# An adaLN block on one core: leads that change over time in the planner that orders all engines

## The chip, the core and the metric

The kernel runs on one core of a Trainium2 chip. The metric is the time of one execution on the device in microseconds (us); lower is better. Before the change three runs took 1426.54, 1429.36 and 1430.04 us, median 1429.36.

The core has five engines that take their own instructions, each in its written order, and wait for one another by semaphores: TensorE (PE; matmuls, with the weight loads shown apart as PEld), VectorE (DVE), ScalarE (ACT), GpSimd (POOL) and SyncE (SP, which issues the DMAs). TensorE writes its results to PSUM, which has eight banks here of 512 fp32 values in each of 128 partitions.

## The reference

For a batch of 8 sequences of 1024 tokens with 128 features, a modulated block: six linear-attention transformer layers between two residual sums, then a feed-forward part with values rounded to fp4.

```python
mod = (_silu(L0_c) @ L0_wmod).reshape(L0_c.shape[0], 6, 1, -1)
sa, ca, ga, sb, cb, gb = (mod[:, 0], ..., mod[:, 5])
ga = (2 * (ga >= 0) - 1) * jnp.maximum(jnp.abs(ga), 0.25)   # gb the same
h = _layernorm(x, axis=-1) * (1 + ca) + sa
x = x + ga * _L0_attn_ref(h, ...)      # six layers
h = _layernorm(x, axis=-1) * (1 + cb) + sb
x = x + gb * _L0_ffn_ref(h, ...)
```

One of the six layers:

```python
xn = _layernorm(x, ln1_w[i], ln1_b[i])
q, k, v = xn @ wq[i], xn @ wk[i], xn @ wv[i]          # 8 heads of 16
q = softmax(q, axis=-1); k = softmax(k, axis=-2)      # k: over the tokens
context = einsum('bhnd,bhne->bhde', k, v)
x = einsum('bhnd,bhde->bhne', q, context) @ wo[i] + bo[i] + x
xn = _layernorm(x, ln2_w[i], ln2_b[i])
hdn = leaky_relu(xn @ w1[i], 0.01)                    # 512 wide
x = hdn @ w2[i] + x
```

The feed-forward part takes its input, its weights and the gated product through a rounding to fp4 in blocks of 16 values with a scale of their own (largest absolute value / 6), then computes `silu(x @ gate.T) * (x @ up.T)`, 352 wide, and the projection back to 128. All matmuls are fp32.

## The kernel before

**Tiles.** One sequence of the batch is a tile of 128 partitions by 8 chunks of 128 features; most steps work on a half of it (4 chunks, 512 columns, one bank of PSUM). Four sequences are in flight at once, each in one of four sets of buffers ("lanes"; sequence b has lane b modulo 4), so sequences 4 to 7 start when 0 to 3 have left their buffers.

**Stages.** For a sequence there are eight stages: 0 is the first normalisation and modulation; 1 to 6 are the layers; 7 is the feed-forward part. A layer (`layer`) does, for each half: statistics of the norm (DVE L559, L561), its reciprocal root by logarithm and exponential on ACT and four small DVE steps (`layernorm`, L575 to L601), the normalised values (DVE L607, ACT L614), transposes on PE (`transposed`, L633), keys and queries (PE L867 and L914), their softmaxes (DVE L874, L923, L930, L943, L950; ACT L890, L937; POOL L955), keys times normalised input (PE L977), two small products (PE L986, L1011), the attention output (PE L1044, added by DVE L1029), and the two matmuls of the layer's own MLP (PE L1063, 512 columns; L1080, 128 columns, accumulated over four).

Stage 7 (`ffn`) normalises, rounds to fp4 (`fp4`: DVE L658 to L701, ACT L690, POOL L708), forms gate and up (PE L1120, ACT L1128 with the silu table, DVE L1136) in four quarters of two chunks, rounds each quarter to fp4, transposes it (PE L1151, ACT L1166), projects it down (PE L1177) and adds it to x (DVE L1186). "Quarter 4.3" below is quarter 3 of sequence 4. Each two quarters end in a store on SP's queue.

**The silu table.** ACT holds the tables of one set of functions. Gates need another set than the exponentials and logarithms of the layers, so each change between the two kinds costs a table load, shown as ACT_TABLE_LOAD at L1128 (to silu) or L1261 (back).

**The order.** The code does not run its steps as it writes them: it records each as a `Step` in a `Plan` (`add`), with its engine, an estimate of its duration and what it reads and writes. `order` then plays the whole program once while it is built. Of all steps whose inputs are there it takes the one that can start first; between steps that can start at the same time it takes the one with the largest sum of its `tail` (the longest chain of work behind it) and its `lead`. The steps are written to the engines in the order so found, and that order is fixed in the program. A step's lead is a number of its stage and sequence, from the table `LEAD` (8 sequences by 8 stages), so `LEAD` decides how the sequences in flight are interleaved. Set-up work that belongs to no stage (weights' preparation, loads, the modulations) has a lead of its own, set by `aside` and `load`.

**The fillers.** Where TensorE would stand idle for over 0.6 us in the played schedule, `order` puts matmuls of the identity by itself there (`warm`, L1250), as many as fit, if a bank of PSUM is free for them. Their result is never read.

```python
pick = (t + cost, -s.tail - s.lead, n, t, cost)
...
gap = e == "PE" and t - free[e] > self.GAP
while gap and min(bank_free) <= free[e]:
```

Of the kernel before, what the change touches and what calls it, by code (L numbers as in the profile page):

```python
# [37 lines left out]
class Buf:  # L38
# [4 lines left out]
    def __init__(self, pool, shape, tag, name, parts=1, dtype=F32):  # L43
        self.tag, self.make, self.tile = tag, (pool, shape, dtype, tag, name), None
        self.parts, self.after = [Part(self, i) for i in range(parts)], None
# [16 lines left out]
class Ps:  # L62


    n = 0
# [17 lines left out]
class Plan:  # L83
# [6 lines left out]

    def __init__(self):
        self.steps, self.wrote, self.read, self.on = [], {}, {}, {}
        self.lead, self.batch = 0.0, -1

    def add(self, eng, occ, fn, r=(), w=(), func=None, port=False):

        s = Step()
        s.eng, s.occ, s.fn, s.func, s.lead = eng, occ, fn, func, self.lead  # L100
        s.batch, s.port = self.batch, port or eng == "POOL"
        s.lat, s.n, s.deps, s.outs = self.LAT[eng], len(self.steps), set(), []
        s.ps = list(dict.fromkeys(x for x in (*r, *w) if isinstance(x, Ps)))
        for x in s.ps:
            x.users += 1

        def keys(things):
            for x in things:
                if isinstance(x, Buf):
                    yield from x.parts  # L110
                else:
                    yield x

        r, w = list(keys(r)), list(keys(w))
        for x in (*r, *w):
            if isinstance(x, Part):
                tag = x.buf.tag
                if x.buf.after is None:
                    x.buf.after = self.on.get(tag, set())
                    self.on[tag] = set()  # L120
                s.deps |= x.buf.after
                self.on[tag].add(s.n)
        for x in (*r, *w):
            if x in self.wrote:
                s.deps.add(self.wrote[x])
        for x in w:
            s.deps.update(self.read.get(x, ()))
        for x in r:
            self.read.setdefault(x, []).append(s.n)
        for x in w:  # L130
            self.wrote[x], self.read[x] = s.n, []
        s.deps.discard(s.n)
        for x in s.ps:


            if x.first is None:
                x.first = s
            else:
                x.first.deps.update(d for d in s.deps if d < x.first.n)
        self.steps.append(s)  # L140

    def order(self, warm):


        steps = self.steps
        for s in steps:
            for d in s.deps:
                steps[d].outs.append(s.n)
        for s in reversed(steps):
            s.tail = s.occ + s.lat + max((steps[o].tail for o in s.outs), default=0.0)  # L150
        free = dict.fromkeys(self.LAT, 0.0)
        free["PE"] = 1.8
        bank_free = [0.0] * BANKS
        left = [len(s.deps) for s in steps]
        ready = [0.0] * len(steps)
        cand = {e: {s.n for s in steps if s.eng == e and not s.deps} for e in free}
        table, port_free = None, 0.0
        out, todo = [], len(steps)
        while todo:
            banks = sorted(bank_free)  # L160
            best = None
            for e, c in cand.items():
                for n in c:
                    s = steps[n]
                    t = max(free[e], ready[n], port_free if s.port else 0.0)
                    need = sum(x.bank is None for x in s.ps)
                    if need:
                        t = max(t, banks[need - 1])
                    if t < INF:
                        cost = SWITCH if s.func and table and s.func != table else 0.0  # L170


                        pick = (t + cost, -s.tail - s.lead, n, t, cost)
                        if best is None or pick < best[1]:
                            best = (e, pick)
            assert best is not None
            e, (_, _, n, t, cost) = best
            gap = e == "PE" and t - free[e] > self.GAP
            while gap and min(bank_free) <= free[e]:
                to = free[e] + (2 if free[e] < self.COLD else 1) * mm(P)  # L180
                if to > t - self.BRINK:
                    break
                w, bank = Step(), bank_free.index(min(bank_free))
                w.fn, w.func = lambda bank=bank: warm(bank), None
                free[e] = bank_free[bank] = to
                out.append(w)
            s, todo = steps[n], todo - 1
            cand[e].discard(n)
            end = t + cost + s.occ
            table = s.func or table  # L190
            port_free = end if s.port else port_free
            for x in s.ps:
                if x.bank is None:
                    x.bank = min(range(BANKS), key=lambda i: bank_free[i])
                    bank_free[x.bank] = INF
                x.users -= 1
                if x.users == 0:
                    bank_free[x.bank] = end + s.lat
            free[e] = end
            for o in s.outs:  # L200
                ready[o] = max(ready[o], end + s.lat + self.SEE[steps[o].eng])
                left[o] -= 1
                if left[o] == 0:
                    cand[steps[o].eng].add(o)
            out.append(s)
        return out
# [21 lines left out]
def mm(n):  # L228

    return 0.01 + n * 1.66e-3  # L230


def move(kb):

    return max(0.45, kb * 4.0e-3)
# [6 lines left out]
def kernel(  # L242
# [38 lines left out]


    LEAD = [
        [1790.16, 1590.63, -133.39, -357.74, -170.79, -746.20, -949.01, -1084.50],
        [-328.73, -887.78, 125.60, 74.06, -1565.69, -372.37, -623.33, -863.15],
        [207.64, -149.66, -1586.32, -941.39, -1592.66, 94.98, -1452.11, -1239.07],
        [-746.08, 404.44, -824.95, -647.90, -118.96, -127.38, -1745.97, -425.45],
        [542.33, -1490.70, -1058.13, -1440.16, -391.61, -339.71, -149.19, -1160.38],
        [-1848.97, 2004.30, 268.43, 1104.45, -662.40, -326.99, -708.65, -1359.47],
        [573.17, -93.03, 284.47, -756.78, -278.27, -748.61, 318.91, -1786.29],  # L290
        [968.46, -558.77, 587.25, -611.65, -410.32, -941.76, -1400.05, -882.04],
    ]
    NQ = 4
    FCOLS = C // NQ * I

# [7 lines left out]
    plan = Plan()  # L303
    add = plan.add

    def stage(b, i):
        plan.lead, plan.batch = LEAD[b][i], b * len(LEAD[b]) + i

    @contextmanager
    def aside(late=40.0):  # L310

        kept = plan.lead, plan.batch
        plan.lead, plan.batch = -late, -2
        yield
        plan.lead, plan.batch = kept

    def chunks(t):
        return t.rearrange("p (c d) -> p c d", d=D)
# [1 line left out]
    def big(ln, which, name):  # L320

        return Buf(lanes_p, [P, W], f"{which}{ln}", name, 2 * H)
# [14 lines left out]

    def load(dst, src, key, kb=64):

        if plan.batch == -1:  # L340
            plan.lead -= 1e4
        add("SP", move(kb), lambda: nc.sync.dma_start(dst(), src), w=key)

# [20 lines left out]
    def load_x(b, h):  # L364
        if h == 0:
            x0s[b] = big(b % LANES, "x0", f"x0_{b}")
        src = x_d[b].rearrange("(p c) d -> p c d", c=C)[:, h * HC : (h + 1) * HC, :]
        load(lambda: chunks(half(x0s[b], h)), src, at(x0s[b], h), 256)
# [10 lines left out]
    for l in range(L):  # L379
# [13 lines left out]
        if l == 0:  # L393
            load_x(3, 0)
            load_x(3, 1)
    plan.lead = 0.0

    ident = const.tile([P, P], F32, name="ident")
    make_identity(nc, ident)
# [689 lines left out]
    def ffn(x, mod, b, ln):  # L1089
# [18 lines left out]
        )  # L1108
        G = C // NQ
        gs = []  # L1110
        for i in range(NQ):
            g = Buf(lanes_p, [P, W], f"{'CDEA'[i]}{ln}", f"g_{b}_{i}", G)
# [88 lines left out]
    for b in range(B):  # L1201
        ln = b % LANES
        stage(b, 0)
        mod = mod_buf(b, ln)
        if b < LANES:
# [5 lines left out]
        with aside():  # L1211
            modulation(mod, b, b < LANES)
        x = big(ln, "X", f"x_{b}")
# [39 lines left out]
    last, table = {}, None  # L1253
# [2 lines left out]
    behind = mybir.DependencyInfo(  # L1256
        mybir.DependencyClass.NoSync, mybir.DependencyReason.DATA
    )
    for step in plan.order(warm):
        if step.func == "exp" and table != "exp":  # L1260
            nc.scalar.preload_act_table_set("natural_log_exp_and_others")  # L1261
        table = step.func or table
        step.fn()
        new = block.instructions[done:]
        done += len(new)
        for i in new:
            if i.engine in last:
                tc.add_manual_dep(i, last[i.engine], behind, reason="order")
            last[i.engine] = i.name
# [40 lines left out]
```

## Time and profile before

| what | value |
|---|---|
| median of three runs | 1429.36 us |
| the profiled execution | 1430.2 us, its span 1428.5 us |
| TensorE busy | 1415.8 us, 9395 passes |
| VectorE / ScalarE / GpSimd busy | 1146.0 / 995.9 / 241.8 us |
| TensorE's clock, mean of what was granted | 0.999 |
| DMA | 18.81 MB, 13 GB/s over the span |

The span runs from the first to the last instruction of the profile, and the execution's own time is 1.7 us longer. An fp32 matmul takes two passes through TensorE, and the trace shows both, so most counts of its rows are twice the number of instructions; a transpose takes one pass. A matmul's own duration in a row runs from its start until its result is written; the next pass starts before that. Line numbers are those of the kernel before; in the changed kernel lines after the new table stand 37 further down.

### The profile page before, as it was taken

What the parts mean: (1) busy time and instruction counts of PE and PEld (TensorE: products, weight loads), DVE (VectorE), ACT (ScalarE), POOL (GpSimd) and SP (SyncE); (2) the same over time, 40 slices, a digit from 0 to 9 for tenths busy, and PEclk for the clock granted to TensorE, in tenths of its full rate; (3) what the DMA queues carried; (4) which work ended last, traced back from release to release, by engine and by line L of the source; (5) the groups of instructions that cost most, each with busy time, mean ns of one, the idle gap of its engine ahead of it and who ended that gap; (6) DMA issues with size and microseconds to landing.
All of it is one profiled execution on the core that took longest, in us unless ns stands there. A gap on an engine that the chain in (4) does not pass through costs nothing.

```text
span 1428.5 us, 26720 instructions
## 1 busy us (share of the span) xinstructions
PE 1415.8 (99%) x9395; PEld 1140.9 (80%) x9395; DVE 1146.0 (80%) x4560; ACT 995.9 (70%) x2280; POOL 241.8 (17%) x207
## 2 busy tenths in 40 slices
PE   9999999999999999999999999999999999999998
PEld 7787877878787887877787788878887877886887
DVE  7896776667787985798978978987796775989986
ACT  5776777566677777676776867785677677777763
POOL 2020101001121220112112212111221001222232
PEclk9999999999999999999999999999999999999999
DMA  7100000000000000000000000100000000000000
GB/s 214 47 1 1 1 1 1 1 1 1 1 22 6 16 1 1 1 27 16 1 1 28 8 1 8 27 1 8 9 1 1 1 1 1 1 16 1 16 16 15
DMA packets 16006, 18.81 MB, mean 13 GB/s; under 512 B 1552, under 2 KB 9848, under 8 KB 15872
## 3 DMA queue, kind: packets, MB, share of 16 engines
q1 hardware_dynamic: 15872, 17.10, 3.8%
q8 instruction: 74, 1.21, 0.3%
q14 instruction: 60, 0.49, 0.1%
HBM read 12.88 MB, written 4.22 MB: 12 GB/s over the span
## 4 chain that ended last, share of the span: by engine, by line
PE 82%; DVE 14%; ACT 2%; issue 1%; POOL 0%; DMA 0%; SPq 0%; DVEq 0%; POOLq 0%
PE ps L1080 23%; PE ps L1063 22%; PE ps L633 10%; PE ps L1044 5%; PE ps L977 5%; PE ps L914 5%; PE ps L867 5%; PE ps L1120 3%; PE ps L1177 2%; PE ps L1151 1%; PE warm L1250 1%; DVE x L1029 1%; DVE stats_m L559 1%; DVE nmax L874 1%; DVE qmax L923 1%; DVE stats_a L559 1%
## 5 line engine op out<-in xcount | busy, mean ns | idle before, releaser
L1063 PE MATMUL ps<-xT_m,w_sb 128*128 128x512 f32 x768 | 350.4, 595 | 1.5 <-ACT xT_m L847 1.4
L1063 PEld LDWEIGHTS ps<-xT_m,w_sb 128*128 128x128 f32 x768 | 137.5, 191 | 133.2 <-issue 91.9
L1029 DVE TENSOR_TENSOR x<-ps,x 128x512 f32<-128x512 f32 x192 | 129.5, 681 | 119.1 <-PE ps L1080 107.6
L955 POOL TENSOR_TENSOR q<-q,qsum 128x512 f32<-128x512 f32 x96 | 102.9, 1079 | 674.8 <-DVE qsum L950 374.6
L1080 PEld LDWEIGHTS ps<-w_sb,hT_D 128*128 128x128 f32 x768 | 103.9, 192 | 17.2 <-issue 13.6
L914 PEld LDWEIGHTS ps<-wq_sb,xT_a 128*128 128x128 f32 x768 | 96.6, 192 | 26.1 <-issue 16.8
L1080 PE MATMUL ps<-w_sb,hT_E 128*128 128x128 f32 x768 | 117.1, 275 | 0.0
L1080 PE MATMUL ps<-w_sb,hT_C 128*128 128x128 f32 x768 | 117.1, 275 | 0.0
L1080 PE MATMUL ps<-w_sb,hT_B 128*128 128x128 f32 x768 | 117.1, 275 | 0.0
L1080 PE MATMUL ps<-w_sb,hT_D 128*128 128x128 f32 x768 | 117.0, 275 | 0.0
L1080 PEld LDWEIGHTS ps<-w_sb,hT_B 128*128 128x128 f32 x768 | 101.4, 192 | 1.2 <-issue 0.7
L614 ACT ACTIVATE xh_a<-x,shift_a,rstd_a 128x128 f32<-128x128 f32 x192 | 83.8, 488 | 25.9 <-DVE shift_a L601 25.4
L1080 PEld LDWEIGHTS ps<-w_sb,hT_E 128*128 128x128 f32 x768 | 101.2, 192 | 0.0
L1080 PEld LDWEIGHTS ps<-w_sb,hT_C 128*128 128x128 f32 x768 | 101.2, 192 | 0.0
L914 PE MATMUL ps<-wq_sb,xT_a 128*128 128x128 f32 x768 | 99.0, 275 | 0.0
L1044 PEld LDWEIGHTS ps<-m,qT 128*128 128x128 f32 x768 | 91.1, 192 | 7.5 <-DVE m L1018 3.1
L867 PE MATMUL ps<-xT_a,wk_sb 128*128 128x512 f32 x192 | 96.7, 599 | 0.4 <-DMA wk_sb<-in_L_attn_wk_dram 0.2
L977 PEld LDWEIGHTS ps<-k,xh_a 128*128 128x128 f32 x768 | 90.7, 192 | 6.1 <-issue 4.5
L1044 PE MATMUL ps<-m,qT 128*128 128x128 f32 x768 | 95.1, 275 | 0.1
L575 ACT ACTIVATE rstd_a<-mv_a,eps 128x4 f32<-128x4 f32 x96 | 28.4, 297 | 93.9 <-DVE mv_a L561 80.4
L977 PE MATMUL ps<-k,xh_a 128*128 128x128 f32 x768 | 93.5, 275 | 0.0
L614 ACT ACTIVATE xh_m<-x,shift_m,rstd_m 128x128 f32<-128x128 f32 x192 | 81.8, 487 | 13.9 <-DVE shift_m L601 13.6
(176 smaller groups left out, 3132.5 us busy)
## 6 DMA issues: line engine op xcount, KB each, us to landing
x<-in_L_attn_x_dram SPq DMA_DIRECT2D x16, 256.0 KB, 3.2
out_dram<-x SPq DMA_DIRECT2D x16, 256.0 KB, 2.0
w_sb<-in_L_attn_w_dram SPq DMA_DIRECT2D x12, 256.0 KB, 3.9
mod<-mod_d SPq DMA_DIRECT2D x8, 256.0 KB, 4.3
mod<-mod_d SPq DMA_DIRECT2D x4, 128.0 KB, 3.3
wmod_b<-in_L_wmod_dram SPq DMA_DIRECT2D x1, 384.0 KB, 4.1
wk_sb<-in_L_attn_wk_dram SPq DMA_DIRECT2D x6, 64.0 KB, 3.0
wq_sb<-in_L_attn_wq_dram SPq DMA_DIRECT2D x6, 64.0 KB, 2.8
```

The costliest lines, as they stand in the source:

```text
L559: nc.vector.bn_stats(stats.ap()[:, c, :], s(c))
L614: nc.scalar.activation(d(c), s(c), AF.Identity, bias=shift.ap()[:, c : c + 1], scale=rstd.ap()[:, c : c + 1],)
L633: nc.tensor.transpose(t.ap()[:, c * P : (c + 1) * P], chunks(half(src, h))[:, c, :], ident)
L867: lambda tk=tk, h=h: nc.tensor.matmul(tk.ap(), wk_sb[:, l, :], half(xT, h), start=True, stop=True),
L914: nc.tensor.matmul(tq.ap()[:, c * D : (c + 1) * D], half(xT, h)[:, c * P : (c + 1) * P], wq_sb[:, l, :], start=True, stop=True,)
L955: lambda h=h, hs=hs: nc.gpsimd.tensor_tensor(heads(half(q, h)), heads(half(q, h)), each(qsum.ap()[:, hs]), ALU.mult),
L977: nc.tensor.matmul(tc_.ap()[:, :D], chunks(xh.ap())[:, c, :], chunks(k.ap())[:, c, :], start=(c == 0), stop=(c == C - 1),)
L1029: lambda: nc.vector.tensor_tensor(half(x, h), t.ap(), half(x, h), ALU.add),
L1044: nc.tensor.matmul(to.ap()[:, c * D : (c + 1) * D], half(qT, h)[:, c * P : (c + 1) * P], m.ap(), start=True, stop=True,)
L1063: lambda th=th, h=h, j=j: nc.tensor.matmul(th.ap(), w1_sb[:, l, j * P : (j + 1) * P], half(xmT, h), start=True, stop=True,),
L1080: nc.tensor.matmul(ty.ap()[:, c * D : (c + 1) * D], hidden(j)[:, c * P : (c + 1) * P], w2_sb[:, l, j, :], start=(j == 0), stop=(j == NJ - 1),)
L1120: lambda t=t, cc=cc, n=n: nc.tensor.matmul(t.ap()[:, :I], hT.ap()[:, cc * P : (cc + 1) * P], wguT[:, n, :], start=True, stop=True,),
```

## The change

The rank of a step no longer takes its lead from when it was recorded. A step keeps its stage, `(b, i)`, and `order` looks up the lead of that stage while it plays. It has a copy of the table, and a second table `TURNS` says at which times of the played schedule which entries take another value: at 15 us, sequence 2's stage 0 drops to -419, and so on in 27 entries up to 1365 us. `LEAD` itself is rounded to whole numbers; besides, sequence 3's stages 0 and 3 rise by 223 and 156, and sequence 4's row drops by 3 to 4. Set-up work without a stage ranks 70 us later than it did (`LATE`), apart from the loads at the start.

Nothing of what is computed changes, and no instruction of the chip is written differently: steps, tiles, buffers and durations in the planner are the same. What changes is the order in which they stand on each engine, the bank of PSUM that each gets, and with them how many fillers and table loads there are.

```diff
-        self.lead, self.batch = 0.0, -1
+        self.lead, self.stage = 0.0, None
...
-    def order(self, warm):
+    def order(self, leads, turns, warm):
...
-        table, port_free = None, 0.0
+        table, port_free, now = None, 0.0, 0.0
+        leads, turns = [list(x) for x in leads], list(turns)
         out, todo = [], len(steps)
         while todo:
+            while turns and turns[0][0] <= now:
+                for b, i, lead in turns.pop(0)[1]:
+                    leads[b][i] = lead
...
-                        pick = (t + cost, -s.tail - s.lead, n, t, cost)
+                        lead = leads[s.stage[0]][s.stage[1]] if s.stage else s.lead
+                        pick = (t + cost, -s.tail - lead, n, t, cost)
...
-            end = t + cost + s.occ
+            now = t + cost
+            end = now + s.occ
...
     LEAD = [
-        [-746.08, 404.44, -824.95, -647.90, -118.96, -127.38, -1745.97, -425.45],
-        [542.33, -1490.70, -1058.13, -1440.16, -391.61, -339.71, -149.19, -1160.38],
+        [-523, 404, -825, -492, -119, -127, -1746, -425],
+        [539, -1494, -1061, -1443, -395, -343, -152, -1163],
...
+    TURNS = [
+        (15, [(2, 0, -419)]),
+        (30, [(1, 0, -1058)]),
...
+        (1215, [(5, 7, -1015), (7, 5, -1033)]),
+        (1260, [(4, 7, -889), (5, 7, -174)]),
+        (1275, [(4, 7, -2229), (5, 7, -1786)]),
+        (1320, [(5, 7, -1788), (6, 7, -1804)]),
+        (1335, [(5, 7, -1863)]),
+        (1350, [(5, 7, -1786), (7, 7, -2743)]),
+        (1365, [(7, 7, -1661)]),
+    ]
+    LATE = 70.0
...
     def aside(late=40.0):
...
-        plan.lead, plan.batch = -late, -2
+        plan.lead, plan.stage = -LATE - late, None
...
-    for step in plan.order(warm):
+    for step in plan.order(LEAD, TURNS, warm):
```

## The prediction

> **What bounds the kernel now.** I read the page's busy shares first, then the chain of waits, then the matmuls grouped by line and shape, and last the windows that say where idle time lies.
>
> ```profile
> span 1428.5 us, 26720 instructions
> PE 1415.8 (99%) x9395; PEld 1140.9 (80%) x9395; DVE 1146.0 (80%) x4560; ACT 995.9 (70%) x2280; POOL 241.8 (17%) x207
> PE 82%; DVE 14%; ACT 2%; issue 1%; POOL 0%; DMA 0%; SPq 0%; DVEq 0%; POOLq 0%
> ```
>
> TensorE is idle for 1428.5 - 1415.8 = 12.7 us. It sets the end, so only two things can shorten the run: fewer passes on TensorE, or less time lost between them. An order changes no useful pass. But not all passes are useful: L1250 multiplies the identity by itself to fill a gap and its result is never read.
>
> ```profile
> L1250 PE MATMUL warm<-ident 128*128 128x128 f32 x388 | 49.8, 282 | 1.6 <-POOL ident masks.py:199 1.6
> ```
>
> The 282 ns is one pass from end to end; passes overlap, so the price is the pitch. The chain of waits in order of time gives it for each shape (start, duration, what):
>
> ```profile
> 1183.20 6.87 PE ps L1063 x16
> 1190.07 7.14 PE ps L1080 x64
> ...
> 1387.84 6.03 PE warm L1250 x54
> ...
> 1415.02 5.14 PE warm L1250 x46
> ```
>
> 6.03 / 54 = 0.1117 us a pass, and two passes a filler (388 records for 194 instructions): 0.2233 us a filler, 388 x 0.1117 = 43.3 us in all. In the same way the chain's rows give 0.1116 us for a useful 128-wide pass (7.14 us for 64 of L1080), 0.4294 for a 512-wide one (6.87 for 16 of L1063), 0.296 for L1120 (2.96 for 10), 0.109 for a transpose (2.18 for 20 of L633). Times the counts by line: 960 x 0.4294 + 5952 x 0.1116 + 256 x 0.296 + 1792 x 0.109 and about 6 of set-up = 1353 us of useful passes. So the span is 1353 useful + 43 filler + 32 of everything else (start, end, stalls). These 75 us are all that an order can touch.
>
> Where they lie, by windows of 50 us, fillers alone (length, PE busy and count, PEld busy and count, clock, DMA, GB/s):
>
> ```profile
> 0.00:50.00 50.00, 21.51 (x162) 20.07 (x162) 1.00 0.61 186
> 550.00:600.00 50.00, 2.86 (x20) 2.67 (x20) 1.00 0.00 1
> 1200.00:1250.00 50.00, 0.61 (x4) 0.53 (x4) 1.00 0.01 1
> 1300.00:1350.00 50.00, 1.28 (x10) 1.20 (x10) 1.00 0.03 11
> 1350.00:1400.00 50.00, 12.41 (x100) 11.93 (x100) 1.00 0.03 12
> 1400.00:1450.00 50.00, 11.09 (x92) 10.75 (x92) 0.99 0.03 11
> ```
>
> Start and tail, then; the middle has ten fillers. One stall of the middle has no filler: around 645 us TensorE waits 2.3 us behind a table load and three gates on ScalarE (L1128), and then runs at half clock:
>
> ```profile
> PE ps L633 <- ACT g L1128: 2.5, 2, 2.3
> ...
> 648.30:651.60 3.30, 3.30 (x6) 1.24 (x5) 2.46 (x4) 1.60 (x3) 2.47 (x3) 0.50 0.02 5
> ```
>
> The 3.3 us at clock 0.50 do 1.7 us of work less, so this stall costs 2.3 + 1.7 = 4.0 us.
>
> **What the Trainium skill says.** "TensorE: Matmul & The Clock Gate", Part 1: the clock halves after an idle window of about 3.4 us, and the windows run free. The trace shows the halving after only 2.3 us of full idleness, so shorter stalls can cost too. "Perfetto Trace Analysis", on the most-contended engine: matmul busy is a poor measure since matmuls are pipelined. The trace agrees: 99% busy hides 75 us, which is why I count passes by pitch. "ScalarE: Activation LUTs", on what a table load costs: about 1.28 us for the load and as much again for a drain; the trace shows 1.283 us for the load in each of its 37.
>
> **The change part by part.** The leads decide ties of the planner, which runs while the program is built; nothing of it runs on the chip. What can be read without a clock is the order of instructions that comes out.
>
> Useful work: the same 5,405 matmul instructions, the same DVE, POOL and SP operations; cost 0. ScalarE has two table loads less (35 for 37): 2.6 us on an engine with 30% idle, counted at nothing since TensorE sets the end; the cover is ScalarE's idle time, and if it is gone at such a place it costs what the stall at 645 us did.
>
> Fillers: 141 instead of 194, by place. Start, up to the 74th useful matmul: 75 for 81, -6. Middle: the ten after matmuls 2266 and 2282, and two after 4743, are gone, -12. Before batch 7's last feed-forward: 20 between matmuls 5125 and 5251 are gone; those after 5321 and 5333 are 14 for 32, together -38. In batch 7's own serial feed-forward: 52 for 49, +3. Sum -6 -12 -38 +3 = -53, and 53 x 0.2233 = 11.8 us less on TensorE.
>
> What takes their place is useful work moved, not created. Before, batches 4 and 5 finish their down projections at matmuls 4954 and 5171. After, quarters 4.1 and 4.2 come 104 and 76 matmuls later, 4.3 comes 259 later, 5.1, 5.2 and 5.3 come 90, 42 and 104 later, between the last layers of batch 7. What is late next at the end is batch 7's own chain of normalise, quantise, gate, quantise, project: 23 fillers in one gap there both before and after. That stays.
>
> Each moved quarter also moves its DVE chain: reduce 0.88, two small scalings 0.18 + 0.19, reciprocal 0.42, three sweeps of 0.88, add 0.42 = 4.7 us, plus 0.8 + 0.6 + 0.4 on ScalarE and 1.4 on POOL. Nothing is added in sum; it stands in windows where DVE is busy 42 to 46 of 50 us. I cost it at nothing, with DVE's idle share there as cover.
>
> DMA: the write of the small first modulation goes out four places earlier on SP's queue, ahead of feed-forward weights needed much later; DMA is idle (0.00 to 0.09 of a window past 50 us), cost 0. The result stores of batches 4 and 5 alternate. Behind a store that waits for 4.3 stands only 5's second one, then 6 and 7; these come later anyway. Cost 0. The 70 us by which set-up work ranks later show as another order of its matmuls (L505, L517) among batch 0's first layer; that is inside the -6.
>
> The unknown is the other 32 us: waits that the planner doesn't fill, because no bank of PSUM was free (645 us) or because they are short. The order doesn't show them. Bounds: -4 if the stall at 645 us isn't met again and no new one arises; +4 if there is another like it (17 of the 18 table loads for gates had none of over 1 us). I take -2, half of the stall.
>
> Sum: -11.8 - 2 = -13.8. The profiled execution took 1430.2 (span 1428.5 and 1.7 around it), which gives 1416.4; the three runs have a median 0.8 lower, 1429.4, so 1415.6. I say 1416.
>
> **The rivals.**
> A, the forecast: fillers leave, useful work closes up. For: TensorE is the bound and pitch is constant. 1416, between 1411 and 1421.
>
> B, the unfilled waits shrink as well. A tighter order lowers both kinds. TensorE's idle time between 50 and 1350 us is 4.3 us by the windows (2.4 of it at 645), the half clock 1.7; with all of it gone, 11.8 + 6 = 17.8 and about one more at the start: 1410. Against: some waits below a microsecond seem to be in any order.
>
> C, waits take the fillers' place. Every engine takes its instructions in the written order, so where data come later than planned, TensorE stands idle instead. For: behind some fillers TensorE idled on, 0.82 us for DVE's L1136 at 1361 us and 0.62 us for ScalarE's L847 at 1365. Seven places lose fillers; 0.6 to 1 us at each gives back 4 to 7: 1422. Against: long stretches of the middle have 50.00 of 50 busy without any filler.
>
> D, slower: DVE becomes the bound of the tail. The four quarters that move furthest (4.1, 4.3, 5.1, 5.3) carry 4 x 4.7 = 18.8 us of DVE. Between 1250 and 1400 us DVE is busy 42.75 + 46.27 + 42.55 = 131.6 of 150, which leaves 18.4. If the moved work came wholly from before 1250 it would fill this, and each further microsecond would delay batch 7's normalisation; if all 18.8 landed on its chain: 1429.4 - 11.8 + 18.8 = 1436. It decides once more than 11.8 us land there. Against: before, these quarters already ran at 1262 to 1338 us, inside the same window, so its sum hardly changes.
>
> **How the numbers follow.** A 0.69, B 0.13, C 0.12, D 0.06. Predicted is A, 1416. Its bounds give 1411 to 1421; B's low side and C's centre are taken in: 1409 to 1423. A measurement here can tell 0.3% (4.3 us) from no change. A and B are faster by more; of C a quarter falls within 0.3%, of D a third. Faster 0.69 + 0.13 + 0.09 = 0.91, same 0.05, slower 0.04.
>
> **What would show it.** The profile of the changed kernel should have 282 filler passes (388 before), PE still at 99%, useful passes at the same pitch, about 8 us less filler time past 1300 us and none in the middle. Each step is wrong if: idle time on TensorE rises by over 4 us (C), DVE between 1250 and 1400 shows no idle and L633 or L1063 wait for it (D), or a gate's table load again leaves TensorE idle with half clock after it (no -2). Useful passes at another pitch would break the whole sum.

## The result, and the profile after

The changed kernel takes 1419.13 us (median of 4 runs, 1418.68 to 1420.5), the kernel before 1429.66 us beside it (4 runs, 1426.54 to 1430.04). The ratio is 0.9933 with a 95% interval of 0.9915 to 0.995: 10.5 us less, where 13.8 were forecast. The profiled span goes from 1428.5 to 1417.8 us.

The page of the changed kernel, its span, busy shares and the chain of waits by engine:

```profile
span 1417.8 us, 26520 instructions
PE 1404.3 (99%) x9289; PEld 1127.9 (80%) x9289; DVE 1151.5 (81%) x4560; ACT 992.6 (70%) x2278; POOL 241.5 (17%) x207
PE 81%; DVE 12%; ACT 3%; DMA 2%; SPq 1%; issue 1%; POOL 1%; POOLq 0%
```

TensorE is still the bound. It is idle for 1417.8 - 1404.3 = 13.5 us (12.7 before), so no idle time was won; all of the gain is in what fills the busy time. Its passes are 106 fewer, and the groups by line show which:

```profile
L1287 PE MATMUL warm<-ident 128*128 128x128 f32 x282 | 36.8, 284 | 1.6 <-POOL ident masks.py:199 1.6
```

They are the fillers: 282 passes where there were 388. By windows of 50 us, fillers alone (length, PE busy and count, PEld busy and count, clock, DMA, GB/s), in the same windows as shown for the kernel before:

```profile
0.00:50.00 50.00, 20.58 (x150) 18.89 (x150) 1.00 0.62 186
550.00:600.00 50.00, 0.00 (x0) 0.00 (x0) 1.00 0.00 1
1200.00:1250.00 50.00, 0.00 (x0) 0.00 (x0) 1.00 0.00 1
...
1350.00:1400.00 50.00, 9.69 (x78) 9.35 (x79) 1.00 0.07 27
1400.00:1450.00 50.00, 6.52 (x54) 6.26 (x54) 0.98 0.03 11
```

Between 1300 and 1350 us there are none now, where there were 10. In sum 12 passes less at the start, 24 in the middle, 70 past 1300 us: with two passes a filler these are the 6, 12 and 35 instructions that the order had shown.

The waits of TensorE by who released them (us in total, times, longest):

```profile
PE ps L670 <- ACT g L1165: 2.3, 1, 2.3
PE warm L1287 <- POOL ident masks.py:199: 1.6, 1, 1.6
PE ps L670 <- DVE xh_a L644: 0.7, 3, 0.3
PE ps L951 <- ACT g L1165: 0.7, 1, 0.7
PE ps L1157 <- ACT g L1165: 0.7, 1, 0.7
```

The first row is the stall that I had half counted out: a transpose behind a table load and three gates, 2.3 us as before, at 640 instead of 645 us. The timeline of the changed kernel at that place (start, duration, engine, what, idle time before it):

```profile
636.51 4.31 PE L1157 MATMUL ps<-wguT,hTf 128*128 128x352 f32 x14
...
641.28 1.28 ACT L1165 ACT_TABLE_LOAD   x1
...
642.58 1.18 ACT L1165 ACTIVATE g<-ps 128x352 f32<-128x352 f32 x3
...
643.10 0.65 PE L670 MATMUL ps<-ident,xh_a 128*128 128x128 f32 x4 [2.28 <-ACT g L1165]
```

The trace of before has the same rows at this place with the same durations, 4.1 us later; the fillers that left ahead of it (6 at the start and 10 below 600 us, 16 x 0.2233) make up 3.6 of these. The input of the transposes is complete when ScalarE begins the table load (its L651 ends just ahead of it), and the row names a gate as releaser: what TensorE waits for is the bank of PSUM that the first gate empties, and the table load stands ahead of that gate. That holds for the last 1.8 of the 2.3 us at least; in the first 0.4 us ScalarE is still writing the input. What is different is the clock after the stall. The window of 3.4 us that follows the stall in the changed kernel (PE, PEld, DVE, ACT, POOL busy, then the clock):

```profile
643.10:646.50 3.40, 3.40 (x14) 1.97 (x14) 3.40 (x6) 2.63 (x5) 2.77 (x2) 1.00 0.00 0
```

1.00, where it was 0.50 before. Whether the change did that is asked by the experiments.

Two readings are left. DVE between 1250 and 1400 us, where the moved quarters land:

```profile
1250.00:1300.00 50.00, 49.69 (x328) 39.95 (x328) 48.62 (x172) 41.88 (x89) 8.03 (x7) 1.00 0.02 7
1300.00:1350.00 50.00, 49.35 (x321) 39.30 (x320) 46.74 (x144) 36.25 (x75) 15.72 (x12) 1.00 0.00 1
1350.00:1400.00 50.00, 48.43 (x322) 39.45 (x321) 42.20 (x107) 26.69 (x57) 15.21 (x11) 1.00 0.07 27
```

137.6 of 150 us, 6.0 more than before and 12.4 short of full. And the end of the chain of waits (start, duration, what): the program still closes with the serial feed-forward of batch 7 and its fillers.

```profile
1390.61 5.00 PE ps L1157 x16
1395.61 3.79 PE warm L1287 x34
...
1401.61 2.68 PE ps L1214 x24
1404.29 5.14 PE warm L1287 x46
...
1411.52 2.69 PE ps L1214 x24
```

### The profile page after: what moved, and what is told of

The parts are those of the page before. It is cut to its first block, busy times and chain, and to the rows that moved or that the text cites. A ratio compares the mean times of both kernels' runs of the same rounds, so it can differ in the third digit from the quotient of the medians.

```text
span 1417.8 us, 26520 instructions
## 1 busy us (share of the span) xinstructions
PE 1404.3 (99%) x9289; PEld 1127.9 (80%) x9289; DVE 1151.5 (81%) x4560; ACT 992.6 (70%) x2278; POOL 241.5 (17%) x207
## 4 chain that ended last, share of the span: by engine, by line
PE 81%; DVE 12%; ACT 3%; DMA 2%; SPq 1%; issue 1%; POOL 1%; POOLq 0%
PE ps L1100 20%; PE ps L1117 19%; PE ps L670 11%; PE ps L1014 6%; PE ps L951 6%; PE ps L904 5%; PE ps L1081 5%; PE ps L1157 4%; PE ps L1214 2%; DVE x L1066 1%; PE ps L1188 1%; DVE stats_a L596 1%; PE warm L1287 1%; DMA w_sb<-in_L_attn_w_dram 1%; DVE stats_m L596 1%
## 5 line engine op out<-in xcount | busy, mean ns | idle before, releaser
L1117 PEld LDWEIGHTS ps<-w_sb,hT_D 128*128 128x128 f32 x768 | 103.9, 192 | 17.2 <-issue 13.2
L1117 PE MATMUL ps<-w_sb,hT_E 128*128 128x128 f32 x768 | 117.1, 275 | 0.0
L1117 PE MATMUL ps<-w_sb,hT_C 128*128 128x128 f32 x768 | 117.1, 275 | 0.0
L1117 PE MATMUL ps<-w_sb,hT_B 128*128 128x128 f32 x768 | 117.1, 275 | 0.0
L1117 PE MATMUL ps<-w_sb,hT_D 128*128 128x128 f32 x768 | 117.0, 275 | 0.0
L651 ACT ACTIVATE xh_a<-x,shift_a,rstd_a 128x128 f32<-128x128 f32 x192 | 83.9, 489 | 29.2 <-DVE shift_a L638 28.5
L1117 PEld LDWEIGHTS ps<-w_sb,hT_B 128*128 128x128 f32 x768 | 101.3, 192 | 1.0 <-issue 0.5
L1117 PEld LDWEIGHTS ps<-w_sb,hT_C 128*128 128x128 f32 x768 | 101.2, 192 | 0.0
L1117 PEld LDWEIGHTS ps<-w_sb,hT_E 128*128 128x128 f32 x768 | 101.2, 192 | 0.0
L651 ACT ACTIVATE xh_m<-x,shift_m,rstd_m 128x128 f32<-128x128 f32 x192 | 82.3, 488 | 16.3 <-DVE shift_m L638 15.8
```

What stands on the lines that cost most here:

```text
L651: nc.scalar.activation(d(c), s(c), AF.Identity, bias=shift.ap()[:, c : c + 1], scale=rstd.ap()[:, c : c + 1],)
L1117: nc.tensor.matmul(ty.ap()[:, c * D : (c + 1) * D], hidden(j)[:, c * P : (c + 1) * P], w2_sb[:, l, j, :], start=(j == 0), stop=(j == NJ - 1),)
```

## The experiments

The question was threefold: is a filler worth its pitch, was the stall at 640 us (and the half clock) in the hands of the change, and does the gain come from the turns or from the other edits. In the table, "rest" is the span of the profiled run less 1353 us of useful passes (11.6 more in `extra_passes`), less filler passes x 0.1117 us.

| kernel | median us (runs) | span | filler passes | rest |
|---|---|---|---|---|
| before | 1429.66 (4) | 1428.5 | 388 | 32.2 |
| before_again | 1429.0 (1) | 1427.3 | 388 | 31.0 |
| changed | 1419.13 (4) | 1417.8 | 282 | 33.3 |
| after_again | 1419.3 (1) | 1417.6 | 282 | 33.1 |
| no_fillers | 1428.04 (20) | 1426.3 | 0 | 73.3 |
| extra_passes | 1429.39 (12) | 1428.1 | 282 | 32.0 |
| static_leads | 1453.02 (4) | 1450.3 | 440 | 48.2 |
| early_turns | 1439.7 (4) | 1438.0 | 414 | 38.8 |
| gates_held | 1454.38 (4) | 1454.2 | 480 | 47.6 |
| stall_repaired | 1416.27 (4) | 1413.7 | 282 | 29.2 |
| order_refined | 1409.76 (4) | 1407.6 | 226 | 29.4 |

### Is a filler only the sign of a wait?

The order stays, but the fillers are not written to TensorE:

```diff
                 free[e] = bank_free[bank] = to
-                out.append(w)
```

> The changed kernel in the same order, with its 141 fillers left out of the program (their place in the played schedule is kept, so the useful instructions stand as they did). Theory (fillers only occupy waits that are there anyway): no gain; TensorE idles 31 us more, and the clock is halved for part of the start and the tail, which costs 2 to 12 us: 1421 to 1431. Rival (fillers themselves hold useful work up, so that fewer of them is the gain as such): up to 31.5 us less, 1388 to 1415.

1428.04 us (1425.97 to 1429.04), 8.9 more than with them; the ratio to before is 0.9992 [0.9985, 0.9999]. The windows of this kernel at start and end show why (engines' busy times, then the clock):

```profile
0.00:50.00 50.00, 31.20 (x132) 20.33 (x133) 39.26 (x230) 28.17 (x73) 10.38 (x18) 0.83 0.61 186
1350.00:1400.00 50.00, 44.34 (x261) 34.00 (x260) 40.28 (x115) 28.57 (x61) 12.65 (x9) 0.93 0.07 27
1400.00:1450.00 50.00, 14.24 (x77) 12.57 (x75) 14.54 (x27) 5.92 (x12) 6.55 (x4) 0.85 0.03 10
```

The passes leave and TensorE simply stands idle in their place; then the clock, which is 1.00, 1.00 and 0.98 in these windows with the fillers, falls to 0.83, 0.93 and 0.85, and the useful passes after the waits take longer. So here a filler does not cost the time it takes: it stands where a wait is anyway, and holds the clock. The gain of the change is therefore not that fillers were dropped but that the waits which called for them are gone; their number only measures these waits.

### Is a pass worth its pitch?

106 transposes more, which write the same values again, two in each of 53 groups. By the order of recording these are the 50 groups of sequence 1 and the first three of sequence 2:

```diff
         t = Ps(psum)
+        Ps.calls = getattr(Ps, "calls", 0) + 1
+        more = [0, 0] if 50 < Ps.calls <= 103 else []
...
         def go():
-            for c in range(HC):
+            for c in [*range(HC), *more]:
```

> The changed kernel, with two more transposes in 53 of its groups of transposes, all of sequence 1 between about 60 and 900 us, where TensorE has no fillers: 106 more passes, each repeating a block that is written anyway, no other change of order. Theory (in the middle TensorE is the bound and a pass costs its pitch): 106 x 0.109 = 11.6 us more, 1430.7, between 1428 and 1433. Rival (waits of others hide them): 1418 to 1423.

1429.39 us (1427.08 to 1430.04), 10.3 more than the changed kernel. In the traces the last matmul starts 10.5 us later than in the repeat of the changed kernel, against 106 x 0.109 = 11.6 by pitch: nine tenths of the price is paid, and 1.1 us disappears in waits that were there. At these places, where TensorE has hardly a gap, an added pass costs nearly its pitch.

### Did the change do anything to the stall?

Both kernels once more, unedited.

> The kernel before once more, for a second profile. Its stall near 645 us (2.3 us behind a table load and three gates) must be there again. Theory (whether the clock halves after so short a stall is a matter of where a free-running window stands): the half clock may be missing this time; in the four other profiles with the same stall it was missing in all. Rival (the stall always brings the half clock in this order): half clock again near 648 us.

> The changed kernel once more, for a second profile. The waits of TensorE of over 0.6 us must stand at the same places as in the first (near 449, 640, 1331, 1351 and 1353 us), if they belong to the order and not to chance. The half clock after 640 us may come or not; if it comes, the span is 1.5 to 2 us longer.

They take 1429.0 and 1419.3 us. Each has the stall again (2.44 and 2.45 us between the starts of two matmuls, beyond the pitch), and the changed kernel's waits near 449, 1331, 1351 and 1353 us are where they were. But the kernel before now runs on at full clock; its window, the one that had shown 0.50:

```profile
648.30:651.60 3.30, 3.30 (x15) 1.86 (x15) 3.30 (x6) 2.06 (x4) 2.47 (x3) 1.00 0.02 5
```

The same program, the same wait, another clock: the half clock belonged to that one execution (the last section says on what it depends). Laying the two traces of before side by side by the number of the pass, fillers included, gives its price: up to pass 4250 the first profile is 0.5 us ahead, from 4280 on 1.2 us behind and constant to the end, so 1.7 us. The forecast had that right as a price and wrong as something that this change removes.

### What makes the stall?

Theory: a bank of PSUM is missing, since the gates of L1157 take them while ScalarE, which empties them, is still at other work. The gates may not take the last three free banks around that place:

```diff
+                    if need and s in self.gates and 632 <= now < 638:
+                        need = min(BANKS, need + 3)
...
                         r=[*at(hT, cc // HC), ("wguT", n)], w=[t],
                     )
+                    plan.gates.add(plan.steps[-1])
```

> The changed kernel, in whose played schedule the matmuls of gate and up may not take the last three free banks of PSUM between 632 and 638 us; nothing else is edited. Theory 1 on the stall (the gates take all eight banks while ScalarE is at other work, so a ready transpose finds none): no wait of TensorE for L1165's gates of over 1 us near 640 us. Theory 2 on the whole (the turns fit only the schedule that they were found on; a small change in it moves everything after, and later turns then do not fit): 240 fillers for 141, 22 us, and unfilled waits of up to 15 us besides: 1439 to 1458. Rival (a stall is worth what it lasts): 2 us less than the changed kernel, 1416 to 1418.

The stall is gone; the window of this kernel (engines' busy times, clock):

```profile
630.00:650.00 20.00, 20.00 (x88) 12.46 (x87) 19.82 (x49) 17.95 (x35) 4.83 (x3) 1.00 0.00 0
```

With the banks kept free the wait is gone; together with the releaser that the trace names, this shows the bank as its cause. But the kernel takes 1454.38 us (ratio 1.0177 [1.016, 1.0194]), 35 more than the changed one: everything that `order` chose after that place is different, 99 fillers more (22.1 us) and 14 us more of other waits. The turns are given as times of the played schedule, and after a small shift they would come at the wrong moments; this reason is argued, the loss is shown.

The same repair without letting the rest move: the order of the changed kernel is written out as a list, 205 of its 6525 steps are put elsewhere, all of them around 590 to 690 us, and `order` plays the list:

```diff
-            while turns and turns[0][0] <= now:
...
+            n = PLAY[len(steps) - todo]
+            s = steps[n]
+            e = s.eng
...
+PLAY = [
```

> Of the changed kernel's 6525 steps, 205 are put at other places, all of them between about 590 and 690 us, among them the three gates that stand behind the table load at 640 us; the rest of the order, and all 141 filler instructions, stay where they are. If a stall is worth just what it lasts, so long as the rest of the order is kept: the wait of 2.3 us is gone, no wait of TensorE of over 1 us is left between 600 and 700 us, 282 filler passes as before, and the time falls from 1419.3 by 2 to 2.5 us, to 1417. If the missing bank only comes back a little later (the rival), a wait of about the same length stands somewhere between 650 and 700 us, and the time stays at 1419 or above.

1416.27 us (1415.42 to 1416.76; ratio to before 0.9913 [0.9896, 0.9929]). The timeline of this kernel shows the matmuls of gate and up that stand ahead of the transposes now in two portions, six passes and four, with the table load beside useful passes:

```profile
634.80 1.94 PE L1157 MATMUL ps<-wguT,hTf 128*128 128x352 f32 x6
...
636.58 2.74 PE L1100 MATMUL ps<-xT_m,w_sb 128*128 128x512 f32 x6
637.60 1.28 ACT L1165 ACT_TABLE_LOAD   x1
638.89 0.82 ACT L1165 ACTIVATE g<-ps 128x352 f32<-128x352 f32 x2
639.41 1.45 PE L1157 MATMUL ps<-wguT,hTf 128*128 128x352 f32 x4
640.70 0.60 PE L670 MATMUL ps<-ident,xh_a 128*128 128x128 f32 x4
```

PE has 49.87 of 50 us busy between 600 and 650 us, 47.63 in the changed kernel. Since all but this stretch is the same order, the n-th pass of both traces, fillers included, can be compared by its start (us):

```
pass      after_again   stall_repaired   difference
300            51.05            49.16        -1.89
3900          586.34           584.41        -1.93
4300          656.33           652.40        -3.93
9000         1373.76          1369.86        -3.90
```

The repair is worth 2.0 us, between 586 and 656 us, and keeps them to the end. The other 1.9 us of this pair come from the first 12 us, where both kernels have the same order (more on it below), so of the 2.9 us by medians 2.0 are the repair's; the other 0.9 is within what executions of one order differ by. With the rest kept in place, removing this stall was worth 2.0 of the 2.4 us that it lasted.

### Turns or table?

The changed kernel without any turn, and with only those below 1215 us:

```diff
-    for step in plan.order(LEAD, TURNS, warm):
+    for step in plan.order(LEAD, [], warm):
```

```diff
-    for step in plan.order(LEAD, TURNS, warm):
+    for step in plan.order(LEAD, [x for x in TURNS if x[0] < 1215], warm):
```

> The changed kernel with its new LEAD rows and LATE, but an empty TURNS: leads never change while the schedule is played. Its program has 220 fillers instead of 141. Theory (a filler stands for a wait of its own length, and the turns replace waits by useful work): 79 fillers x 0.2233 us = 17.6 us more than the changed kernel, about 1437 us, between 1432 and 1442. Rival 1 (the new rows and LATE bring the gain, the turns nothing): 1417 to 1423. Rival 2 (the gain is the half clock that the profile of before had and that of the changed kernel had not): 1419 to 1423, with no half clock in its trace.

> The changed kernel with the turns before 1215 us alone; the seven later entries are left out, so the order up to there is that of the changed kernel and the tail is not steered. 207 fillers for 141, all 66 more of them in the last 200 us. Theory: 66 x 0.2233 = 14.7 us more than the changed kernel, 1434 us, between 1429 and 1438, and up to 1215 us a trace like that of the changed kernel, with the same stall near 640 us. Rival 1 (the early turns bring the gain): 1417 to 1423. Rival 2 (a bound of DVE in the tail, which deferring work makes worse): below 1419.

`static_leads`: 1453.02 us, ratio 1.0166 [1.0151, 1.0181], and 11 above the top of what I expected. Its 440 filler passes are 17.6 us more than in the changed kernel; the other 15 are in the rest, which I had taken for constant. The waits of TensorE in this kernel:

```profile
PE ps L670 <- ACT xT_m L884: 2.6, 2, 2.1
PE ps L670 <- ACT kT L927: 2.5, 3, 1.8
PE ps L670 <- ACT g L1165: 2.5, 2, 2.3
PE ps L1100 <- ACT xT_m L884: 1.7, 3, 0.9
```

Three kinds of waits near 2 us, where the changed kernel has one. A worse order has more of both kinds of waits, those that get fillers and those that don't. The new `LEAD` and `LATE` alone are thus worse than the old ones by 23.5 us; they gain only together with the turns. The two were not run apart, nor the turns with the old table.

`early_turns`: 1439.7 us, ratio 1.0072 [1.0055, 1.0089], 1.7 above the top of what I expected. The turns below 1215 us bring 13.3 of the 33.9 us between `static_leads` and the changed kernel, the last seven the other 20.6. 132 filler passes more are 14.7 of these. The rest is one stall, in the timeline of this kernel:

```profile
1286.16 2.53 PE L1157 MATMUL ps<-wguT,hTf 128*128 128x352 f32 x8
1289.16 1.66 ACT L651 ACTIVATE xh_m<-x,shift_m,rstd_m 128x128 f32<-128x128 f32 x4 [0.39 <-DVE shift_m L638]
1290.83 1.28 ACT L1165 ACT_TABLE_LOAD   x1
1292.12 1.53 ACT L1165 ACTIVATE g<-ps 128x352 f32<-128x352 f32 x4
...
1292.64 3.61 PE L670 MATMUL ps<-ident,xh_m 128*128 128x128 f32 x16 [3.94 <-ACT g L1165]
```

It looks like the pattern of 640 us: the row names a gate, and the transposes start once ScalarE has loaded its table and emptied a bank. But ScalarE writes input of such transposes until 1290.8 us (L651), so the bank accounts for the last 1.8 us of this wait for certain; what the first 2.1 us waited for is not shown. Here the half clock did follow; the window after it:

```profile
1292.60:1295.90 3.30, 3.26 (x16) 3.26 (x17) 3.11 (x7) 3.01 (x6) 0.00 (x0) 0.51 0.00 0
```

3.9 us of wait and about 1.6 of slow passes: with 14.7 this is 20.2 of 20.6.

### Is there a better order?

If the order is all, a better one must beat the changed kernel with the same steps. As in `stall_repaired` the order is a list, here with single steps of the changed kernel's order put elsewhere all over the program, chosen by the planner's own estimates of durations. The list has 6525 numbers; the rest of the edit is that of `stall_repaired`:

```diff
+PLAY = [
...
```

> The changed kernel's order with single steps put at other places all over the program, the same work. 113 filler instructions instead of 141, which at 0.2233 us is 6.3 us less. If the fillers and the stall at 640 us are all that comes off, 1419.3 - 6.3 - 2.3 = 1410.7. If the short unfilled waits (some 29 us of the changed kernel in sum, start and end among them) shrink as well, down to 1407. The rival: data come later than planned where the order has lost its slack, and TensorE stands idle in many short waits instead; then 1414 to 1421, and a long stall with half clock behind it would put it above that.

1409.76 us (1409.35 to 1412.56), ratio to before 0.987 [0.9855, 0.9885]: 9.4 us below the changed kernel. Its fillers and its longest waits:

```profile
L1287 PE MATMUL warm<-ident 128*128 128x128 f32 x226 | 32.1, 290 | 1.8 <-POOL ident masks.py:199 1.6
```

```profile
PE ps L670 <- DVE xh_a L644: 1.8, 2, 1.2
PE warm L1287 <- POOL ident masks.py:199: 1.6, 1, 1.6
PE ps L1214 <- ACT gT L1203: 0.8, 2, 0.6
```

56 passes less are 6.3 us, and the rest falls by 3.9. From one matmul's start to the next, less the pitch of its shape, 14.7 us are lost outside the first 50 us where the first profile of the changed kernel lost 17.7: 3.0 less, of which the stall is 2.4. The remaining 0.9 lies at the start, where executions of one order differ by as much. The rival came in small: one new wait of 1.2 us for DVE (L644, at 54 us). The idle time is not exhausted: 54.6 us of this span are still fillers and rest.

## Why the prediction was right, and where not

1416 us was forecast, between 1409 and 1423, and 1419.1 was measured.

**The fillers, -11.8: right.** 282 passes were counted, with the split by place, and useful passes kept their pitch (7.14 us for 64 passes, 0.1116 each, at L1080 before and at the same line, L1117, after). `extra_passes` confirms the price from the other side. What I wrote loosely as "less on TensorE" needs the reading of `no_fillers`: the fillers themselves cost nothing, the waits below them do.

**"I take -2, half of the stall": failed.** This is the step that was wrong, in two ways. The stall of 2.3 us did not go: it costs 2.44 us beyond the pitch in both kernels. Counted in useful matmuls, the three gates and what stands around them are at the same places in both orders, so the two orders could have told that this wait is met again, contrary to the sentence that the order doesn't show it. The half clock, 1.7 us, was indeed absent afterwards, but that was luck: the repeat of the unedited kernel was without it as well. The two first profiles differ by 10.7 us, and 1.7 of these are this luck.

**The other waits, taken as unchanged: mis-sized.** The time lost from one matmul's start to the next, less the pitch of its shape (0.1116, 0.4294, 0.296 and 0.109 us as in the forecast, other shapes by their median), is 14.1 us outside the first 50 us in `before_again` and 17.5 in `after_again`: +3.4. Some of it lies in new waits of 0.7 to 0.8 us at 449, 1331, 1351 and 1353 us, and 1.5 us between 750 and 800. In the first 50 us 6.5 are lost where it was 7.8, -1.3; executions of one order differ there by up to 1.9, so this part may be chance. -11.8 + 3.4 - 1.3 = -9.7, which is the difference of the spans of these two. Against the forecast of -13.8 the terms that were off are thus -2 (in truth 0 for the stall) and the short waits, which had no term and came to +3.4, with -1.3 at the start against them.

**Rivals.** B (unfilled waits shrink too) is refuted for this change, they grew; `order_refined` shows that they can shrink. C (waits take the fillers' place) took part with 3.4 of the 4 to 7 us that it named, though only partly at the fillers: those at 449 us and between 750 and 800 stand where none had been. D (DVE the bound of the tail) did not come: 6.0 us landed in the window against the 11.8 from which it would have decided, and no wait of TensorE for DVE is above 0.3 us, except one of 0.6.

**What was costed at nothing** held for DMA, which shows no wait past the start, and not wholly for the others. Of the four new waits, three are for ScalarE by the trace (gates L1165 at 449 and 1331 us, the copy L1203 at 1351) and one for DVE (L644 at 1353), so their idle shares were not a full cover. The two table loads less on ScalarE leave no trace of their own. The drain that the forecast named beside a table load does not show: in 31 of the changed kernel's 35 loads the next activation starts 1.29 to 1.30 us after the load's start.

## What to carry to other kernels

Where one engine bounds the kernel and only the order changes, count what the order adds or removes on that engine, times its pitch, and leave a term for short waits that the planner does not see: here 3.4 us came back in one order, and 3.0 went in another. A long stall is gone only if the instructions around it have moved, which the two orders tell. A table of leads, priorities or times fits the schedule on which it was found: half of it, or a small shift, cost 20 to 35 us here, while moving a few steps in a fixed order kept what it gained. Bank-holding matmuls should not be issued so far ahead that all banks wait for one engine that still has a table to load.

## What was not expected of the hardware

**Whether a half clock follows a stall of 2.3 us depends on where the stall lies on a grid of 3.41 us.** Nine profiles have a stall of 2.3 to 2.5 us beyond the pitch. Half clock followed in the first of before and in `gates_held` (at 1251 us), and not in `before_again`, `after_again`, the changed kernel, `extra_passes`, `early_turns` and `no_fillers` near 640 to 650 us, nor in `static_leads` at 662 us. The traces record when the clock changes, and in each of them these times lie whole multiples of 3.413 us apart: in before 9.96, 648.26, 651.67 and 1429.91 us, which is 187, 1 and 228 steps. Where the grid lies differs between executions (the first change comes between 6.29 and 11.55 us). The step ahead of the half clock in before, and the two steps that share the same stall in `before_again` (PE, PEld, DVE, ACT, POOL busy, then the clock):

```profile
644.85:648.26 3.41, 1.13 (x7) 0.79 (x7) 3.41 (x7) 3.35 (x7) 1.08 (x1) 1.00 0.00 0
```

```profile
643.02:646.43 3.41, 2.43 (x9) 1.17 (x7) 3.41 (x9) 2.64 (x6) 0.00 (x0) 1.00 0.00 0
646.43:649.85 3.42, 2.12 (x8) 1.26 (x9) 3.42 (x8) 3.29 (x6) 2.18 (x2) 1.00 0.00 0
```

In before one step holds the whole stall and TensorE is busy for 1.13 us of it; in `before_again` a boundary cuts the stall in two. So it went in all eleven profiles: of 4539 steps at full clock up to the last matmul, the seven in which TensorE was busy for 1.4 us or less were all followed by half clock, two of the four with 1.47 to 1.57 us were, and none of the others. The changed kernel's stall, with 1.47 us in the step from 639.34 us, stood at this edge. So what a kernel has in hand is how long it stalls; where the grid lies is luck. The Trainium skill, "TensorE: Matmul & The Clock Gate", Part 1, has a window of about 3.4 us that runs free of what the kernel does; the grid agrees with that, while a halving after 2.3 us is earlier than the idle time it gives.

**The first 12 us differ between executions of one order.** The timelines of TensorE there, `after_again`:

```profile
5.73 2.05 PE L828 MATMUL ps<-wmod_b,cT 128*128 128x256 f32 x4 [0.74 <-DMA wmod_b<-in_L_wmod_dram]
7.71 2.73 PE L484 MATMUL ps<-wmod_b,cT 128*8 128x512 f32 x4
```

and `stall_repaired`, with the same instructions:

```profile
5.50 1.99 PE L828 MATMUL ps<-wmod_b,cT 128*128 128x256 f32 x4 [0.50 <-DMA wmod_b<-in_L_wmod_dram]
7.41 1.46 PE L484 MATMUL ps<-wmod_b,cT 128*8 128x512 f32 x4
```

The four passes of L484 take 2.73 or 1.46 us: at the start TensorE runs at half speed (in both traces fillers come 0.21 us apart at 3 to 4.5 us, 0.11 from 12 us on), and for how long differs. The first change of the clock is recorded at 11.05 us in `after_again` and at 7.30 in `stall_repaired`, and 3.75 us more at half speed are 1.9 us. (The record begins with this change, which is why windows print 1.00 for the time ahead of it.) By pass 30 the two are 1.89 us apart, and stay so up to the repair. The same page says that the slow stretch at a start varies from run to run, and this trace agrees. Together with the half clock's 1.7 us this is as much as single runs of one kernel differ by (1426.54 to 1430.04 for before), and a reason to compare traces by the n-th instruction where the order is the same.
